# Batch 0 wholly by halves, one piece of zeros less, whole late stores, and a planner that may wait: a two-layer kernel on one core

## The chip, the cores and the metric

One Trainium2 chip; the program runs on one core of it. The time is device microseconds (us) of an execution; of several runs the median is given. The engines are called PE (TensorE, matrix products; PEld is its weight load), DVE (VectorE), ACT (ScalarE), POOL (GpSimd) and SP (SyncE, which here only starts transfers).

## What is computed

Eight batches of 256 tokens by 1024 features, all fp32. The first layer's weight matrix differs from batch to batch: a shared matrix plus a sign matrix, made of an integer mask, times the batch's coefficient. The second layer has one matrix for all batches and adds for each batch a low-rank adapter, chosen by the batch's number. Both layers have a bias and a residual.

```python
def _L0_cond_ref(hidden_states, W, b, coeff, mask):
    output = jnp.einsum('bsi,oi->bso', hidden_states, W) + b
    sign = (2 * mask - 1).astype(hidden_states.dtype)
    diff = jnp.einsum('bsi,bio->bso', hidden_states, sign)
    return output + diff * coeff[:, None, None]
...
def _L1_cond_ref(x, adapter_mapping, W, b, lora_As, lora_Bs):
    base_out = jnp.einsum('bti,oi->bto', x, W) + b
    A = lora_As[adapter_mapping]
    Bm = lora_Bs[adapter_mapping]
    lora_h = jnp.einsum('bti,bir->btr', x, A)
    lora_out = jnp.einsum('btr,bro->bto', lora_h, Bm)
    return base_out + lora_out * SCALING
x = x + _L0_cond_ref(x, L0_cond_W, L0_cond_b, condB_coeff, mask_Bx4096x4096_ik1)
x = x + _L1_cond_ref(x, itok_B_0_23, L1_cond_W, L1_cond_b, L1_cond_lora_As, L1_cond_lora_Bs)
```

Here x is 8 x 256 x 1024, the masks are 8 x 1024 x 1024 int32, and the adapters have rank 16.

## The kernel before, in words

Features lie on the 128 partitions, tokens in the free dimension. A weight matrix of 1024 x 1024 is cut into eight chunks of 128 input features (NC = 8) and two halves of 512 outputs (OH = 512).

**Batch 0** goes straight through, chunk by chunk. For each chunk SP loads the mask and the shared weights (lines 438 to 446) and parts of x (447 to 450); ACT makes the scaled signs of the mask (`convert`, line 403), DVE adds the identity for the residual into one 128 x 128 block and then the shared weights (`add`, line 314), and PE multiplies (line 494): 8 products of 256 columns per chunk. An fp32 product is two passes of PE, each with its weight load, so a chunk is 16 passes and the stage 128. Chunks 0 to 4 (`BY_HALF = 5`) are loaded, converted and added in halves of 512 outputs; for chunk 0 the first half is converted and added in quarters. Chunks 5 to 7 are taken whole: 512 KB per transfer, 1024 columns per conversion and per sum. The host lays the arrays of the chunks that go by halves so that each half is one contiguous piece.

**Batches 1 to 7** use Strassen's seven products with Winograd's sums (`seven`, products on line 680): weights in blocks (`block`, lines 403, 415 and 569), sums of blocks on DVE (line 314) and of tokens (line 665), the bias with the read of the accumulator on ACT (line 591). For batch 1 ACT first shifts the shared weights (line 415), and DVE multiplies the mask in (line 569).

**The second layer** runs for batches 0 to 3 after batch 3 and for batches 4 to 7 after batch 7 (`second_layer`), with seven outer times seven inner products (line 891) and the adapter's down and up products (lines 935 and 966). The first group keeps sums of weights in DRAM, and the second loads them again. Outputs are stored by POOL in the first group and by SP in the second. In the last group (`tail`) `store_halves` cuts a 256 KB store in two: for the four tiles of `c22`, and for the first tile of the last outer product (`done`). The last product of all is cut into three pieces (line 1062), each summed and stored at once.

**Before the first product** PE multiplies zeros (`idle`, lines 346 to 353): 256 and 128 columns, then a product of one row that spreads the coefficients over the partitions (line 362), then 256, 256 and 128 columns (line 368).

**The order of work** on the engines comes from a planner (class `Plan`). Each task has an engine, a guessed duration and perhaps a due time; PE's tasks keep the order in which they are written, and their nominal times add up in `plan.pe`. From these each task gets a latest start `ls`. `order` then simulates the engines: for every engine but PE it takes, of the tasks that can start now, the one with the smallest `ls`. For DVE and ACT (`idle` is true for these two alone) it also looks at tasks that become able while this one would run: if one of them is more urgent and this one is not due for over 3 us (`FAR`), it takes a shorter task that fits in front or waits:

```python
soon = [
    (u, v)
    for u, v in able
    if s < u < s + k.busy + self.MARGIN
    and v.ls < k.ls
    and v.ls < u + self.TIGHT
]
if soon and idle[e] and k.ls > s + self.FAR:
```

The transfers of the start have a fixed rank and so go out in the order in which they are written. The batch numbers (`itok`, 32 bytes) are loaded by SP; POOL reads them when it loads the adapters (line 847).

Of the kernel before, what the change touches and what calls it, by code (L numbers as in the profile page):

```python
# [9 lines left out]
I32 = mybir.dt.int32  # L10
# [3 lines left out]
P = 128  # L14
OH = 512
CG = 2
OQ = 256
BY_HALF = 5
DENSE = (0,)
EARLY = (1,)  # L20
SCALING = 2.0
# [32 lines left out]
class Plan:  # L54
# [60 lines left out]
    def order(self, slots, idle):  # L115
# [41 lines left out]
        while len(out) < len(self.tasks):  # L157
            best = None
            for e in free:
                if e == "PE":  # L160
                    if pe_at == len(pe) or pe[pe_at].open:
                        continue
                    k = pe[pe_at]
                    s = start(k)
                    if s is None:
                        continue
                    c = (s, k.ls, k)
                else:
                    able = [(s, k) for k in ready[e] if (s := start(k)) is not None]
                    if not able:  # L170
                        continue
                    t0 = min(s for s, _ in able)
                    s, k = min(((s, k) for s, k in able if s <= t0 + 0.02), key=lambda c: (c[1].ls, c[1].n))
# [4 lines that stand above are left out]
                        and v.ls < k.ls  # L178
                        and v.ls < u + self.TIGHT
                    ]  # L180
                    if soon and idle[e] and k.ls > s + self.FAR:
                        u = min(soon, key=lambda c: c[0])[0]
                        short = [
                            (a, v) for a, v in able if a <= t0 + 0.02 and a + v.busy <= u - self.MARGIN
                        ]
                        if short:
                            s, k = min(short, key=lambda c: (c[1].ls, c[1].n))
                        else:
                            s, k = min(soon, key=lambda c: (c[1].ls, c[1].n))
                    c = (s, k.ls, k)  # L190
                if best is None or c[:2] < best[:2]:
                    best = c
            if best is None:
                raise RuntimeError(
                    f"no place: {[(e, [k.n for k in v][:9]) for e, v in ready.items()]} at {free}, PE {pe_at}"
                )
            s, _, k = best
            e = k.engine
            for b in k.bufs:
                if b.kind and b.slot is None:  # L200
                    p = pick(b)
                    places[b.kind].remove(p)
                    b.slot = p[1]
            free[e] = s + k.busy
            end = s + k.busy + k.tail
            if k.bytes:
                lane = lanes["SW" if e == "POOL" else "HW"]
                at = max(s + k.busy + 0.5 * self.LATENCY[e], pipe)
                pipe = at + k.bytes / self.RATE
                end = pipe + 0.5 * self.LATENCY[e]  # L210
                lane.pop(0)
                lane.append(end)
            k.end = end
            for b in k.bufs:
                b.left -= 1
                b.end = max(b.end, end)
                if not b.left and b.kind:
                    places[b.kind].append([b.end + self.WAKE, b.slot, not b.partial])
            if e == "PE":
                pe_at += 1  # L220
            else:
                ready[e].remove(k)
            for a in k.after:
                a.open -= 1
                wake = 0.0 if a.engine == e and not k.bytes else self.WAKE
                a.ready = max(a.ready, (s + k.busy if a.engine == e and not k.bytes else end) + wake)
                if not a.open and a.engine != "PE":
                    ready[a.engine].append(a)
            out.append(k)
            k.done = True  # L230
            k.due = s
# [4 lines left out]
def kernel(  # L236
# [109 lines left out]
    def idle(*columns):  # L346
        def emit():
            for n in columns:
                nc.tensor.matmul(
                    idle_ps.t[:, 0, :n], lhsT=zeros[:, :P], rhs=zeros[:, :n], start=True, stop=True  # L350
                )

        pe(1, sum(columns) / 290, emit, (), (idle_ps((0,)),))
# [11 lines left out]
        (h_sb(h_rows), lb_pad((0, 1))),  # L365
        (c_ps((0,)),),
    )
    idle(T, T, T // 2)
    plan.pe = 5.2
    for o, f in ((two_c, 2.0), (neg_c, -1.0)):  # L370
        dve(
# [17 lines left out]
    def parts(c):  # L389
        every = slice(0, OH)  # L390
        if c == 0:
            return [(0, slice(0, OQ)), (0, slice(OQ, OH)), (1, every)]
        return [(0, every), (1, every)] if c < BY_HALF else [(None, every)]

    def halves(o):
        return tuple(q for q in range(2) if o.start < (q + 1) * OQ and o.stop > q * OQ)
# [21 lines left out]
        )  # L418

    w_b0 = [big(f"w_0_{c}", 2, OH) for c in range(NC)]  # L420
    w0_keys = lambda c, h: ((c, h),)

    def w_part(c, i, o):
        keys = tuple((i2, q) for i2 in (ALL if i is None else (i,)) for q in halves(o))
        sel = slice(0, 2) if i is None else slice(i, i + 1)
        return w_b0[c](keys, lambda t: t[:, sel, o])

    def w0_part(c, i, o):
        keys = tuple((c, i2, q) for i2 in (ALL if i is None else (i,)) for q in halves(o))
        sel = slice(0, 2) if i is None else slice(i, i + 1)  # L430
        return w0_sb(keys, lambda t: t[:, c, :].rearrange("p (h o) -> p h o", h=2)[:, sel, o])

    def first_loads(*load):
        k = dma(*load)
# [1 line left out]

    every = slice(0, OH)
    for c in range(NC):
        for i, o in [(0, every), (1, every)] if c < BY_HALF else [(None, every)]:
            n = P * (o.stop - o.start) * 4 * (1 if i is not None else 2)  # L440
            w = w_part(c, i, o)
            as_int = w.buf(w.keys, lambda t, f=w.index: f(t).bitcast(I32))
            src = lambda a: part(a, i)[:, o] if i is not None else a
            sel = lambda r: r if i is None else r.buf(r.keys, lambda t, f=r.index: f(t)[:, 0])
            for r, a in ((sel(as_int), mask[0, c]), (sel(w0_part(c, i, o)), w0T[c])):
                first_loads("SP", r, src(a), n)
            if c < 2 and i == 0:
                first_loads(("ACT", "SP")[c], x0_ref(0, c), part(x0T[0], c), P * T * 4)
            elif c and c % CG == 0 and i in (0, None):
                first_loads("SP", x0_ref(c // CG), x0T[c // CG], P * CG * T * 4)  # L450

    plan.task(
# [6 lines left out]
        due=4.2,  # L459
    )  # L460

    ident_keys = ((0,),)
    plan.task("POOL", 1.2, 0.1, lambda: make_identity(nc, ident.t), (), (ident((0,)),), due=6.0)

    def identity(c):
# [5 lines left out]
    for c in range(NC):  # L471
        h, q = divmod(c * P, OH)
        for i, o in parts(c):
            w = w_part(c, i, o)
            m = w.buf(w.keys, lambda t, f=w.index: f(t).bitcast(I32))
            n = (2 if i is None else 1) * (o.stop - o.start)
            convert(w, m, 0, n)
            if c >= 1 and i in (h, None) and o.start <= q < o.stop:
                d = w_b0[c](((h, q // OQ),), lambda t, h=h, q=q: t[:, h, q : q + P])
                add(d, d, ident((0,)), P)  # L480
            add(w, w, w0_part(c, i, o), n)
    for c in range(NC):
        for i, o in parts(c):
            ots = [
                h * TPH + j
                for h in (ALL if i is None else (i,))
                for j in range(o.start // P, o.stop // P)
            ]
            w = w_part(c, i, o)

            def emit(c=c, ots=ots):
# [49 lines left out]

    for ot in range(1, NC):
        read_dense(ot)
    dma("SP", itok_sb((0,)), itok, 32, due=50.0, ahead=20.0)

# [313 lines left out]
    def second_layer(group):  # L861
# [60 lines left out]
                due=plan.pe + due,  # L922
            )

        def store_halves(o, *where):
            for half in [slice(c, c + 1) for c in range(CG)] if tail else [slice(0, CG)]:
                store(o.buf(o.keys, lambda t, f=o.index, h=half: f(t)[:, h]), *where, c=half)

        def down():
            ph = bank(f"psh_{group}", 2, T, partial=True)  # L930

# [62 lines left out]
        class Run:  # L994
# [10 lines left out]

            def done(self, *uv):
                if self.dest:
                    whole = self.n + 1 < len(OUTER) or uv != (0, 0)
                    (store if whole else store_halves)(self.out[uv], *self.dest, *uv)
                if self.then:  # L1010
                    self.then(uv)

# [161 lines left out]
        for u in range(2):  # L1174
            o2, x2 = (q[u, 0].buf(ALL) for q in (c22, e1))
            add(o2, o2, x2, 1024, due=plan.pe + 5.0)
            for v in range(2):
                store_halves(c22[u, v], 1, 1, u, v)
        k.x2()
        k.y()  # L1180
        k.x3()
# [99 lines left out]
```

## Time and profile before

| what | value |
|---|---|
| three runs | 399.1, 399.93, 399.79 us; median 399.79 |
| the profiled execution | 399.8 us, span 398.1 |
| PE busy | 394.1 us (99%), 2752 passes |
| DVE, ACT, POOL busy | 327.7 (82%), 142.6 (36%), 44.5 us (11%) |
| batch 0's products (line 494) on the chain | 28.93 us, from 5.90 |
| batches 1 to 3 and 4 to 7 (line 680) on the chain | 75.04 us from 34.84, 100.05 us from 202.53 |
| transfers | 84.64 MB, mean 213 GB/s |

The page of the profile tells of one execution. Its chain of waits follows the work that ended last backwards: each step names an engine and a line of the kernel, or a transfer. The timeline lists instructions in order of time, like ones merged; a bracket holds the idle time of the engine ahead of an instruction and what ended it. A row of the windows view gives a stretch, its length, then busy us and instruction count of PE, PEld, DVE, ACT and POOL, PE's granted clock (1.00 is full), the share of time in which the transfer engines were busy, and GB/s. Matmuls overlap and their ends are modelled, so PE's pace is read from the starts.

### The profile page before, as it was taken

Reading aid. Unit: us, or ns where it says so; the run is one execution under the profiler, and the core shown is the slowest. Engines: PE = TensorE matmul, PEld = TensorE weight load, DVE = VectorE, ACT = ScalarE, POOL = GpSimd, SP = SyncE. Lnnn points to the kernel's source line nnn. Section 1 sums busy time; section 2 is a strip of 40 time slices with the busy share of each in tenths; the row PEclk is TensorE's granted clock in tenths of the full one; section 3 lists DMA queues with packets and bytes.
Section 4 is the critical chain, followed back from the end, with each engine's and each line's share of the span. In section 5 each row is a group of like instructions: output and inputs, shape, how many; then the busy total and the mean of one; then the engine's idle time right before and its main releaser. Section 6 shows DMA issues by size and latency. Waiting matters only on the chain.

```text
span 398.1 us, 6970 instructions
## 1 busy us (share of the span) xinstructions
PE 394.1 (99%) x2752; PEld 362.4 (91%) x2752; DVE 327.7 (82%) x417; ACT 142.6 (36%) x253; POOL 44.5 (11%) x87
## 2 busy tenths in 40 slices
PE   8999999999999999999999999999999999999997
PEld 7889999999978888888899999999998888888886
DVE  3559999999999999898999999999737366476475
ACT  5676675612043021017417366472212231110200
POOL 0000000132335331230233000000000000000000
DMA  7999998551558389679589665120001358555844
GB/s 278 395 403 410 406 408 341 179 193 53 194 197 283 150 281 344 209 246 323 174 303 335 198 227 192 53 54 28 0 28 54 115 151 243 173 143 182 272 125 160
DMA packets 31685, 84.64 MB, mean 213 GB/s; under 512 B 4388, under 2 KB 6308, under 8 KB 31652
## 3 DMA queue, kind: packets, MB, share of 16 engines
q1 hardware_dynamic: 25922, 67.19, 49.3%
q0 software_dynamic: 5440, 16.80, 11.3%
q8 instruction: 22, 0.36, 0.4%
q10 hardware_dynamic: 290, 0.20, 0.2%
q14 instruction: 11, 0.09, 0.1%
HBM read 64.25 MB, written 19.92 MB: 211 GB/s over the span
## 4 chain that ended last, share of the span: by engine, by line
PE 98%; DMA 1%; DVE 0%; SPq 0%; issue 0%; DVEq 0%
PE bank L680 44%; PE bank L891 42%; PE bank L494 7%; PE bank L966 2%; PE bank L935 2%; DMA w<-w0T 1%; PE bank L1062 0%; DVE big L314 0%; SPq L327 0%; DVEq L314 0%
## 5 line engine op out<-in xcount | busy, mean ns | idle before, releaser
L314 DVE TENSOR_TENSOR big<-big,big 128x1024 f32<-128x1024 f32 (+1 forms) x104 | 116.7, 1139 | 6.9 <-PE bank L680 4.4
L680 PE MATMUL bank<-small,big 128*128 128x128 f32 x896 | 103.3, 275 | 0.0
L680 PEld LDWEIGHTS bank<-small,big 128*128 128x128 f32 x896 | 101.7, 192 | 0.0
L314 DVE TENSOR_TENSOR big<-bank,big 128x512 f32<-128x512 f32 (+2 forms) x103 | 68.5, 677 | 37.3 <-PE bank L891 30.7
L891 PE MATMUL bank<-small,small 128*128 128x256 f32 x384 | 89.0, 380 | 0.0
L891 PEld LDWEIGHTS bank<-small,small 128*128 128x128 f32 x384 | 72.9, 190 | 10.6 <-issue 0.8
L680 PE MATMUL bank<-big,big 128*128 128x128 f32 x672 | 78.3, 275 | 0.0
L680 PEld LDWEIGHTS bank<-big,big 128*128 128x128 f32 x672 | 76.8, 192 | 0.1
L403 ACT ACTIVATE big<-big,neg_c,two_c 128x1024 f32<-128x1024 int32 (+2 forms) x62 | 69.5, 1162 | 12.3 <-DMA big<-mask 12.0
L314 DVE TENSOR_TENSOR big<-big,w 128x1024 f32<-128x1024 f32 (+2 forms) x62 | 67.4, 1117 | 5.8 <-ACT big L403 3.1
L591 ACT ACTIVATE big<-bank,b 128x128 f32<-128x128 f32 x112 | 32.0, 369 | 75.7 <-PE bank L680 66.2
L891 PE MATMUL bank<-big,small 128*128 128x256 f32 x224 | 52.5, 380 | 0.0
L891 PEld LDWEIGHTS bank<-big,small 128*128 128x128 f32 x224 | 42.4, 190 | 6.2 <-ACT big L318 0.7
L318 ACT COPY bank<-bank 128x512 f32<-128x512 f32 x20 | 11.4, 570 | 87.2 <-PE bank L891 61.8
L318 ACT COPY big<-bank 128x512 f32<-128x512 f32 x32 | 17.6, 593 | 56.7 <-PE bank L891 30.6
L494 PE MATMUL bank<-small,big 128*128 128x256 f32 x128 | 28.9, 390 | 0.2 <-DVE big L314 0.2
L494 PEld LDWEIGHTS bank<-small,big 128*128 128x128 f32 x128 | 25.1, 197 | 4.0 <-DVE big L314 0.5
L314 DVE TENSOR_TENSOR small<-big,small 128x512 f32<-128x512 f32 x35 | 23.8, 686 | 5.7 <-PE bank L891 5.6
L891 PE MATMUL bank<-big,big 128*128 128x256 f32 x112 | 26.7, 381 | 0.0
L891 PEld LDWEIGHTS bank<-big,big 128*128 128x128 f32 x112 | 21.1, 190 | 3.4 <-ACT big L318 0.7
L314 DVE TENSOR_TENSOR small<-big 128x512 f32<-128x512 f32 x21 | 14.4, 686 | 1.5 <-PE bank L891 1.5
L314 DVE TENSOR_TENSOR small<-big,big 128x512 f32<-128x512 f32 x21 | 14.4, 686 | 1.1 <-PE bank L891 1.1
(46 smaller groups left out, 163.9 us busy)
## 6 DMA issues: line engine op xcount, KB each, us to landing
big<-mask SPq DMA_DIRECT2D x59, 512.0 KB, 7.8
big<-xT SPq DMA_DIRECT2D x14, 512.0 KB, 5.8
big<-w1T SPq DMA_DIRECT2D x8, 512.0 KB, 5.5
leaf_S_s<-small POOLq DMA_DIRECT2D x16, 256.0 KB, 3.5
outT<-big POOLq DMA_DIRECT2D x16, 256.0 KB, 3.9
small<-leaf_S_s SPq DMA_DIRECT2D x16, 256.0 KB, 2.7
leaf_A_s<-small POOLq DMA_DIRECT2D x12, 256.0 KB, 2.7
leaf_S_a<-big POOLq DMA_DIRECT2D x12, 256.0 KB, 2.7
```

Of the source, the lines that this page charges most:

```text
L314: return dve(lambda: f(o.ap(), x.ap(), y.ap()), n, (x, y), (o,), due)
L318: "ACT", n / 1200 + 0.06, 0.11, lambda: nc.scalar.copy(o.ap(), x.ap()), (x,), (o,), due
L403: lambda: nc.scalar.activation(o.ap(), x.ap(), AF.Identity, bias=neg_c.t[:, b : b + 1], scale=two_c.t[:, b : b + 1]),
L494: nc.tensor.matmul(dense[ot // 2].t[:, ot % 2, :], lhsT=w_b0[c].t[:, h, j * P : (j + 1) * P], rhs=x0[c // CG].t[:, c % CG, :], start=c == ...
L591: lambda o=o, p=p, bias=bias: nc.scalar.activation(o.ap(), p.ap(), AF.Identity, bias=bias.ap()),
L680: nc.tensor.matmul(ps[:, j, :], lhsT=l[:, c, j * P : (j + 1) * P], rhs=m[:, 2 * a + c, :], start=first and a == 0 and c == 0 and j == 0, s ...
L891: nc.tensor.matmul(ps.t[:, j, :], lhsT=lt[:, c, j * P : (j + 1) * P], rhs=rt[:, c, :], start=start and c == 0 and j == 0, stop=False, skip ...
L935: nc.tensor.matmul(ph.t[i * S : i * S + R, 0, :], lhsT=la.t[:, i, c, :], rhs=y[GB * group + i, c // TPH].t[:, c % TPH, :], start=c == 0, s ...
L966: nc.tensor.matmul(ps[b].t[:, j, :], lhsT=lb_pad.t[rows, o : o + P], rhs=h_sb.t[rows, :], start=j == 0, stop=j == 1, skip_group_check=True,)
```

## The change

Five edits. Chunks 5 to 7 of batch 0 are taken by halves like the others, in the loads, the conversions, the sums and the layout that the host makes. The second series of zeros ends 128 columns earlier. The load of the batch numbers is issued by POOL. The stores that were cut in two go out whole. And the planner gets one more case: when the most urgent task k that could start now is due within 3 us, but a more urgent one becomes able while k would run, would be late behind k, and can itself be done before k is due, then the engine (DVE or ACT) waits for it.

```diff
-BY_HALF = 5
...
+                    late = [(u, v) for u, v in soon if v.ls < s + k.busy and u + v.busy <= k.ls]
+                    if late and idle[e] and k.ls <= s + self.FAR:
+                        s, k = min(late, key=lambda c: (c[1].ls, c[1].n))
-                    if soon and idle[e] and k.ls > s + self.FAR:
+                    elif soon and idle[e] and k.ls > s + self.FAR:
...
-    idle(T, T, T // 2)
+    idle(T, T)
...
-        return [(0, every), (1, every)] if c < BY_HALF else [(None, every)]
+        return [(0, every), (1, every)]
...
     for c in range(NC):
-        for i, o in [(0, every), (1, every)] if c < BY_HALF else [(None, every)]:
...
+        for i in range(2):
+            w = w_part(c, i, every)
+            m = w.buf(w.keys, lambda t, f=w.index: f(t).bitcast(I32))
+            first_loads("SP", m, part(mask[0, c], i), P * OH * 4)
+            first_loads("SP", w0_part(c, i, every), part(w0T[c], i), P * OH * 4)
...
-    dma("SP", itok_sb((0,)), itok, 32, due=50.0, ahead=20.0)
+    dma("POOL", itok_sb((0,)), itok, 32, due=50.0, ahead=20.0)
...
-        def store_halves(o, *where):
-            for half in [slice(c, c + 1) for c in range(CG)] if tail else [slice(0, CG)]:
-                store(o.buf(o.keys, lambda t, f=o.index, h=half: f(t)[:, h]), *where, c=half)
-
...
-                    whole = self.n + 1 < len(OUTER) or uv != (0, 0)
-                    (store if whole else store_halves)(self.out[uv], *self.dest, *uv)
+                    store(self.out[uv], *self.dest, *uv)
...
-                store_halves(c22[u, v], 1, 1, u, v)
+                store(c22[u, v], 1, 1, u, v)
...
-    for k in range(BY_HALF):
+    for k in range(D // P):
         by_part(arrays["mask"][0, k])
         by_part(arrays["w0T"][k])
```

More of the change, by code (lines that the diff above doesn't have):

```diff
@@ L420 @@
     w_b0 = [big(f"w_0_{c}", 2, OH) for c in range(NC)]
-    w0_keys = lambda c, h: ((c, h),)
     def w_part(c, i, o):
-        keys = tuple((i2, q) for i2 in (ALL if i is None else (i,)) for q in halves(o))
-        sel = slice(0, 2) if i is None else slice(i, i + 1)
-        return w_b0[c](keys, lambda t: t[:, sel, o])
+        return w_b0[c](tuple((i, q) for q in halves(o)), lambda t: t[:, i, o])
     def w0_part(c, i, o):
-        keys = tuple((c, i2, q) for i2 in (ALL if i is None else (i,)) for q in halves(o))
-        sel = slice(0, 2) if i is None else slice(i, i + 1)
-        return w0_sb(keys, lambda t: t[:, c, :].rearrange("p (h o) -> p h o", h=2)[:, sel, o])
+        return w0_sb(
+            tuple((c, i, q) for q in halves(o)),
+            lambda t: t[:, c, :].rearrange("p (h o) -> p h o", h=2)[:, i, o],
+        )
     def first_loads(*load):
@@ L438 @@
     for c in range(NC):
-        for i, o in [(0, every), (1, every)] if c < BY_HALF else [(None, every)]:
[L440 to L447, printed above, removed]
+        for i in range(2):
[3 more added lines that the diff above has]
+            first_loads("SP", w0_part(c, i, every), part(w0T[c], i), P * OH * 4)
+            if c < CG and i == 0:
                 first_loads(("ACT", "SP")[c], x0_ref(0, c), part(x0T[0], c), P * T * 4)
-            elif c and c % CG == 0 and i in (0, None):
+            elif c % CG == 0 and i == 0:
                 first_loads("SP", x0_ref(c // CG), x0T[c // CG], P * CG * T * 4)
@@ L460 @@
     )
-    ident_keys = ((0,),)
     plan.task("POOL", 1.2, 0.1, lambda: make_identity(nc, ident.t), (), (ident((0,)),), due=6.0)
@@ L475 @@
             m = w.buf(w.keys, lambda t, f=w.index: f(t).bitcast(I32))
-            n = (2 if i is None else 1) * (o.stop - o.start)
+            n = o.stop - o.start
             convert(w, m, 0, n)
-            if c >= 1 and i in (h, None) and o.start <= q < o.stop:
+            if c >= 1 and i == h and o.start <= q < o.stop:
                 d = w_b0[c](((h, q // OQ),), lambda t, h=h, q=q: t[:, h, q : q + P])
@@ L483 @@
         for i, o in parts(c):
[L484 to L488, printed above, removed]
+            ots = [i * TPH + j for j in range(o.start // P, o.stop // P)]
             w = w_part(c, i, o)
```

## The prediction

> **What bounds the kernel.** I read the chain of waits first, since it says which engine sets the end. Its columns are start, duration (both us) and what.
>
> ```profile
> 0.86 0.38 SPq L327
> 1.30 4.00 DMA w<-w0T
> 5.42 0.43 DVE big L314
> 5.90 28.93 PE bank L494 x128
> 34.84 75.04 PE bank L680 x672
> ...
> 393.51 1.77 PE bank L1062 x12
> 395.28 0.02 issue
> 395.30 0.29 DVE big L314
> ```
>
> From 5.90 to 395.28 the chain never leaves TensorE (PE). Ahead of it stand one transfer of weights that lands at 5.30 and one VectorE (DVE) sum; behind it one sum of 0.29, a store issued at 395.62 that lands at 397.19, and the closing steps up to 398.13. An edit therefore gains only if it makes PE start earlier, stop less, run faster, or shortens those last 2.8 us. The view of PE's waits names 0.2 us on data in the whole run. Weight loads wait 1.3 us in all, in four places, for ScalarE (ACT) copies; there successive matmuls start 0.30 apart instead of 0.216, so all four cost 4 x 0.09 = 0.4 us.
>
> So is anything left in PE's own time? The windows view counts matmul passes per stretch (a pass that crosses a border counts in both); a product has two passes.
>
> ```profile
> 6.90:7.90 1.00, 1.00 (x4) 0.80 (x3) 0.62 (x1) 0.58 (x1) 0.00 (x0) 1.00 1.08 389
> 8.90:9.90 1.00, 1.00 (x7) 0.87 (x6) 0.58 (x2) 0.74 (x1) 0.00 (x0) 1.00 1.04 377
> ```
>
> In narrow timeline windows, passes of 256 columns start at 4.61 and 5.04 (zeros), then 5.90, 6.49, 6.92, 7.34, 7.77 (batch 0), 0.43 apart, and from 8.12 on 0.216 apart. PE runs at half speed until about 8.05, while the column of granted clock says 1.00 throughout. The five passes from 5.90 to 8.12 take 2.22 us instead of 5 x 0.216 = 1.08, which loses **1.1 us**, the one sizeable loss in PE's 389 us. At the end of this stage PE lags behind its data, as these rows show for the last three chunks:
>
> ```profile
> 20.58 1.24 ACT L403 ACTIVATE big<-big,neg_c,two_c 128x1024 f32<-128x1024 int32 x1 [1.13 <-DMA big<-mask]
> 22.18 1.23 DVE L314 TENSOR_TENSOR big<-big,w 128x1024 f32<-128x1024 f32 x1
> 25.38 1.23 DVE L314 TENSOR_TENSOR big<-big,w 128x1024 f32<-128x1024 f32 x1 [0.66 <-DMA w<-w0T]
> 28.87 1.23 DVE L314 TENSOR_TENSOR big<-big,w 128x1024 f32<-128x1024 f32 x1
> ```
>
> Chunks 5, 6 and 7 are ready at 23.41, 26.61 and 30.10. PE takes 16 x 0.216 = 3.46 us per chunk and ends the stage at 34.84, so it begins them at 24.5, 27.9 and 31.4: each lies ready 1.1 to 1.3 us before its turn.
>
> **The parts.** The sum is made on the profiled execution, 399.8 us, of which 398.1 are span and 1.7 lie around it; the median of the three runs shown is 399.79 (399.1 to 399.93).
>
> *Chunks 5 to 7 by halves.* Loads: six transfers of 512 KB become twelve of 256 KB. SP issues six more, 0.33 us each, 2.0 us in all; but its 256 KB issues already stand 0.67 apart (13.21, 13.89, 14.58), waiting for earlier transfers, so issuing stays hidden. The windows view shows 395 GB/s in 14.9 to 20.0 (256 KB pieces) and 405 in 20 to 25 (512 KB). Moving 3.15 MB at the one rate instead of the other takes 7.97 against 7.78, so what is queued behind comes 0.2 us later. That is batch 1's masks and x. ACT: two conversions of 0.81 for one of 1.24, three times, +1.14 us. DVE: two sums of 0.69 for one of 1.23, three times, +0.45 us. Behind these in the queues are ACT's four 1.13 us weight shifts from 28.42 and DVE's mask products (1.28 each, from 30.02). The second of them ends at 33.76 and PE wants it at 36.46, so 2.7 us of cover stand against 0.2 + 0.45 + 1.14 = 1.8. Cost zero. The gain is zero too: a half chunk comes about 0.6 us earlier to an engine already 1.1 us behind. Without that cover the three costs would be paid in part, 0.45 (DVE alone) to 1.8.
>
> *One piece of zeros less.* It removes the passes started at 5.04 and 5.25. The weights land at 5.30 and their sum ends at 5.85, so these passes were not in the way of the product at 5.90: no direct gain. But PE then idles from 5.04 instead of 5.47 until 5.90: a gap of 0.86 instead of 0.43, just before the speed doubles. No row shows what gap the speed-up bears. In the trace, zeros restart at 3.17 after a broken stretch and full speed comes at 8.05, 4.9 us on. The upper bound is that the count starts anew at 5.90: full speed at 10.8, and the 2.75 us between at half speed, **+1.4 us**. The lower bound is zero: less activity gives no reason for an earlier speed-up. I take zero, since the nearest row, the break at 5.47 to 5.90, did not keep full speed from coming at 8.05; I keep both ends.
>
> [...]
>
> *The wait in the planner.* It holds DVE or ACT idle for a more urgent task instead of running one that is due within 3 us. What is held back is that task and everything behind it on the engine. DVE has no idle time to give between 34.8 and 127, as the windows show (DVE is the fourth number):
>
> ```profile
> 34.80:70.00 35.20, 35.20 (x318) 35.20 (x317) 34.83 (x35) 21.93 (x39) 0.00 (x0) 1.00 0.97 385
> 70.00:110.00 40.00, 40.00 (x360) 39.97 (x359) 39.90 (x52) 12.08 (x32) 12.51 (x23) 1.00 0.46 159
> ```
>
> The cover is DVE's lead. I matched the semaphore counts that products wait for with the times they were reached: between 35 and 110 most operands are ready 2 to 5 us before PE's turn; the closest are 0.9 (at 81.1), 1.1 (at 106.1) and 1.9 (at 47.2). One wait is at most the postponed task plus 0.3: 1.23 + 0.3 = 1.5 us of idle time. From below: PE has no waits to be cured but the 0.4 us named above. I take zero, because one short wait of 0.3 to 0.7 fits into the leads.
>
> *Late outputs whole.* Five pairs of 128 KB stores of the last group become five stores of 256 KB: five SP issues of 0.33 fewer, between 383 and 393. SP's last issues (393.14, 394.27, 394.86, 395.62) each come 0.02 after their own sum, so SP's time there is free. A 256 KB store lands 2.1 to 2.9 us after issue; issued at 390.8 it is done by 393.8, before the last store goes out at 395.62. Zero; without that cover a few tenths.
>
> *Batch numbers on GpSimd.* SP loses one issue of 0.30 at 32.47, GpSimd gains one (nearest row: a 4 KB load, 0.49, landing after 3.1). GpSimd waits 76.0 us until 77.4 and reads the numbers first then. Even issued behind the memset there, at 78.4, they would land at 81.5; the adapters' first product is at 113.3. Zero either way.
>
> Sum: 0 + 0 + 0 + 0 + 0, so **399.8**.
>
> **Rivals.** *A: no change that counts.* Chance 0.50. Small signs either way (0.2 on loads, 0.4 on copies) leave 399.1 to 400.5.
>
> *B: slower through the gap in the zeros*, ending on the other side. Place: PE, 5.04 to 5.90. It decides if the speed-up does not tolerate 0.86 us of idle time where it tolerated 0.43. Price 1.4: 401.2, by the bounds 400.6 to 401.6. For it: the break at 2.3 to 3.2 (between the first zeros and the restart at 3.17) is as long, and no full speed came within 4 us of the first zeros at 0.90. Against it: products at 5.90 follow at once and are activity themselves. Chance 0.28.
>
> *C: slower through DVE's order*: halves and new waits use up the closest lead, 0.9. Price: 0.45 + 0.2 + 1.5 - 0.9 = 1.25, or 401.0; more waits, up to 402. Chance 0.11.
>
> *D: faster.* If full speed comes earlier in the run, PE would reach chunk 5 about 1.1 us earlier, the moment it is ready; whole chunks would then hold PE back and halves would not. With the zeros out of the way of an early landing too, 1.1 is gained: 398.7, 398.3 to 399.0. For it: the runs shown spread by 0.8 us, and little but the start can vary. Against it: nothing in the diff hastens the start of this trace. Chance 0.11.
>
> *That the change does not do what it says*: the new condition may hold nowhere, and then the order of DVE and ACT stays. That is inside A.
>
> **How the numbers follow.** About 0.2% (0.8 us) is what a measurement of this kernel can tell from no change. Faster is D, 0.11; same is A, 0.50; slower is B and C, 0.39. The forecast is A's 399.8, whose own range is 399.1 to 400.5. The range of 8 in 10 takes in A and B and most of D: 398.7 to 401.6, leaving out C's far end and D's.
>
> **What would show it.** A: PE's chain again runs from about 5.9 to 395.3 with the batch 0 stage at 28.9 us. B: matmul passes still 0.43 apart after 8.5, and a batch 0 stage of 30 us or more. C: PE waits on DVE between 35 and 127, with idle time of DVE under the same lines. D: passes 0.216 apart before 7 us. The tail is right if the last store again goes out 0.02 after the last sum. What would make me wrong most cheaply is a first transfer that lands at another time than 5.30: it moves the end one for one.

## The result and the profile after

| | before | after |
|---|---|---|
| median of 22 executions each | 399.60 us | 400.27 us |
| lowest and highest | 399.02, 400.06 | 399.40, 401.74 |
| ratio, 95% interval | | 1.0019 (1.0012 to 1.0027) |
| profiled execution, span | 399.8, 398.1 us | 399.95, 398.0 us |

The changed kernel is slower by 0.7 us at the median, yet the profiled execution shows a span 0.1 us shorter. So the profile alone, read as before, explains nothing, and I begin with what it does show. The chain of waits of the changed kernel (start, duration, what; the kernel's lines have moved, and batch 0's products are now line 486, the sums line 316):

```profile
3.24 2.00 PE bank L351 x4
5.24 29.09 PE bank L486 x128
34.34 75.04 PE bank L672 x672
...
116.41 7.10 PE bank L883 x32
123.51 0.04 issue
123.55 1.99 PE bank L883 x8
...
395.09 0.02 issue
395.11 0.29 DVE big L316
```

PE still sets the end. In this execution the first weights landed 0.8 us earlier (at 4.52) than in the execution I had read before, so the first product starts at 5.12; that is luck. The stage of batch 0 takes 29.09 us on the chain, before 28.93. At 123.55 something new stands: PE's products start 0.42 us apart instead of 0.216, so 0.2 us is lost, and its weight load waits for a DVE sum. The first line is the kernel before, whose chain has no break there, the second the changed kernel's timeline:

```profile
116.91 8.83 PE bank L891 x40
```

```profile
123.55 1.59 PEld L883 LDWEIGHTS bank<-small,big 128*128 128x128 f32 x8 [0.44 <-DVE big L316]
```

Two windows of the changed kernel (columns as before):

```profile
8.90:9.90 1.00, 1.00 (x6) 0.87 (x5) 0.60 (x3) 0.81 (x1) 0.00 (x0) 1.00 1.03 393
34.80:70.00 35.20, 35.20 (x317) 35.20 (x317) 34.83 (x34) 22.83 (x39) 0.00 (x0) 1.00 0.98 389
```

DVE is as full as before, ACT works 0.9 us more in the second, and passes run at full speed in the first (0.216 us apart). The halves do what the edit says, two conversions and two sums per chunk (chunk 7's sums):

```profile
27.87 0.69 DVE L316 TENSOR_TENSOR big<-big,w 128x512 f32<-128x512 f32 x1 [1.12 <-ACT big L405]
...
29.94 0.69 DVE L316 TENSOR_TENSOR big<-big,w 128x512 f32<-128x512 f32 x1
```

**Where the time went** is seen when each execution's time is split into its span and what lies around it. I pool the executions of the changed kernel (the 22 above and the 11 of the first rerun below), and 99 of the kernel before, measured beside the experiments. Means: before 399.63 = 397.97 + 1.66, after 400.36 = 398.26 + 2.09 (rounded). Of the 0.73 us, **0.43 lie around the span and 0.29 in it**. Around the span, the kernel before has 1.61 to 1.71 in every execution; the changed one has over 1.85 in 18 of 33, up to 3.24. The prediction took the 1.7 us as a constant.

### The profile page after: what moved, and what is told of

It reads as the page before. It is cut to its first block, busy times and chain, and to the rows that moved or that the text cites. A ratio compares the mean times of both kernels' runs of the same rounds, so it can differ in the third digit from the quotient of the medians.

```text
span 398.0 us, 6960 instructions
## 1 busy us (share of the span) xinstructions
PE 394.1 (99%) x2750; PEld 361.5 (91%) x2750; DVE 328.0 (82%) x420; ACT 144.0 (36%) x256; POOL 45.1 (11%) x88
## 4 chain that ended last, share of the span: by engine, by line
PE 99%; DVE 0%; issue 0%
PE bank L672 44%; PE bank L883 42%; PE bank L486 7%; PE bank L954 2%; PE bank L923 2%; PE bank L351 1%; PE bank L1049 0%; PE bank L364 0%; DVE big L316 0%
## 5 line engine op out<-in xcount | busy, mean ns | idle before, releaser
L405 ACT ACTIVATE big<-big,neg_c,two_c 128x1024 f32<-128x1024 int32 (+2 forms) x65 | 71.1, 1123 | 10.7 <-DMA big<-mask 10.6
```

Source lines behind the costliest of these rows:

```text
L405: lambda: nc.scalar.activation(o.ap(), x.ap(), AF.Identity, bias=neg_c.t[:, b : b + 1], scale=two_c.t[:, b : b + 1]),
```

## The experiments

Each ran in 7 to 12 executions beside 29 to 35 of the kernel before. "Around" is the time less the span.

### One edit alone, on the kernel before

**Zeros.** `idle(T, T, T // 2)` becomes `idle(T, T)`.

> The kernel before with one edit alone: the second series of zeros ends 128 columns earlier. Theory T (the longer gap ahead of the first product makes PE's full speed come later in a part of the executions): ratio 1.001 to 1.003, with some executions 1 to 1.5 us above the rest and batch 0's products taking 30 us or more in those. Rival R1 (the added time comes from GpSimd's early transfer) and rival R2 (it comes from the planner's new order on DVE): ratio 1.000, within 0.0007.

Ratio 1.0010 (1.0001 to 1.0019); mean span 398.39, around 1.73 (at most 1.81). T's size fits, but its sign is absent: no group of executions stands 1 us above the rest (399.48 to 400.72 without a break). In the profile batch 0's products took 29.9 us, but began 0.7 us earlier than in the profile before. And 0.24 us were lost at 197.7, where PE waits for a DVE sum that the planner had put elsewhere: changing the guessed length of the zeros moved DVE's order too. The same order, with the same 0.24 us, stands in the profile of the kernel with the zeros in fewer products below.

**Batch numbers.** `dma("SP", itok_sb...` becomes `dma("POOL", itok_sb...`.

> The kernel before with one edit alone: GpSimd issues the load of the batch numbers. T and R2: ratio 1.000, within 0.0007. R1: 1.001 to 1.002, of which the larger part lies around the span, since the changed kernel's runs show up to 3.2 us around the span where the profiled ones show 1.7.

Ratio 1.0006 (0.9998 to 1.0015), around 1.61 to 1.71: R1's sign is absent. GpSimd issues the load at 1.6 us, since nothing stands ahead of it, and it delays nothing visible. The execution profiled here shows another thing: full speed came at 7.0 us instead of 8.05, and then PE was held back by whole chunks.

```profile
23.95 3.32 PEld L494 LDWEIGHTS bank<-small,big 128*128 128x128 f32 x16 [0.42 <-DVE big L314]
...
28.21 6.77 PEld L494 LDWEIGHTS bank<-small,big 128*128 128x128 f32 x32 [0.94 <-DVE big L314]
```

The brackets are the weight loads' idle time at chunks 5 and 6; between matmul starts 0.2 and 0.7 us were lost. That is the mechanism of rival D: full speed came early and whole chunks held PE back.

**Planner.**

```diff
+                    late = [(u, v) for u, v in soon if v.ls < s + k.busy and u + v.busy <= k.ls]
+                    if late and idle[e] and k.ls <= s + self.FAR:
+                        s, k = min(late, key=lambda c: (c[1].ls, c[1].n))
-                    if soon and idle[e] and k.ls > s + self.FAR:
+                    elif soon and idle[e] and k.ls > s + self.FAR:
```

> The kernel before with one edit alone: the planner's new case. T and R1: ratio 1.000, within 0.0007. R2: 1.0005 or more; the trace shows a matmul start 0.4 instead of 0.216 after the one before it, waiting for DVE between 35 and 130 us, as at 123.55 in the changed kernel, where it costs 0.2 us. If the order holds the same waits as before, 1.000 for R2 too.

Ratio 0.9998 (0.9989 to 1.0007), after 10 us no stall of PE that the kernel before does not have. Alone it costs nothing.

**Halves.** `BY_HALF = 5` becomes `BY_HALF = 8`.

> The kernel before with one edit alone: chunks 5 to 7 of batch 0 by halves too. All three theories: ratio 1.000, within 0.0007; the operands of batch 1's products are ready up to 1 us later than before against their turn, and PE still does not wait. If whole chunks held PE back in executions in which its full speed comes early, 0.999.

Ratio 1.0007 (0.9998 to 1.0015), span 398.27, within what was expected and not told apart from nothing. PE waited 0.08 us at 81.1 and 0.07 at 124.0.

**Whole stores.** `if tail else [slice(0, CG)]` becomes `if False else [slice(0, CG)]`.

> The kernel before with one edit alone: the five halved stores of the last group go out whole. All theories: ratio 1.000 within 0.0007, the last store again issued 0.02 us after the last sum. If whole stores delay the last small ones on the transfer engines, 1.0005 or more, with the last store landing later than 1.6 us after its issue.

Ratio 1.0016 (1.0008 to 1.0025), mean span 398.52: a clear miss, by an edit that I had costed at nothing. What the expectation's last sentence allowed for came true. From the last sum's end to the end of the span it takes 2.96 us, before 2.54. At the end SP waits for the stores to land. This is its view of waits from 394 us on, first of the kernel before, then of this one (waits in total, their number, the longest):

```profile
SPq L327 <- DVE big L314: 1.6, 3, 0.7
SPq L1276 <- DMA outT<-big: 0.7, 3, 0.3
```

```profile
SPq L327 <- DVE big L314: 1.6, 3, 0.7
SPq L1276 <- DMA outT<-big: 1.1, 3, 0.6
```

Two things make it longer. The last 64 KB store lands 1.69 us after its issue instead of 1.57 (1.65 to 1.66 in the changed kernel). And SP tests the eight semaphores of its transfers one after another, 0.06 us each, always in the same order; every transfer takes the next of the eight in turn. Before, the last store happened to hold the eighth, and all others had been tested when it landed. With five transfers fewer it holds the third, and five tests follow: 5 x 0.06 = 0.3. All 14 profiles fit this within 0.03 us:

| version | transfers of SP, against before | last store's place | last sum to end of span |
|---|---|---|---|
| halved stores: before, zeros, planner, two more below | 0 | 8th | 2.53 to 2.54 us |
| batch numbers | -1 | 7th | 2.59 |
| halves | +6 | 6th | 2.66 |
| whole stores | -5 | 3rd | 2.96 |
| changed kernel (+6 - 1 - 5), and its versions | 0 | 8th | 2.62 to 2.63 |
| changed kernel, batch numbers by SP | +1 | 1st | 3.02 |

So the step costs 0.06 for each place short of the eighth, and whole stores cost 0.09 to 0.12 besides. In the changed kernel the places cancel by chance and only the 0.09 is left.

### The changed kernel again, and without one edit

> The changed kernel itself, once more, to be measured beside three versions that each lack one edit. Theory S (the edits cost a little each, mostly by the start: zeros 0.001, halves and batch numbers 0.0007 and 0.0006, planner nothing): ratio 1.0015 to 1.0025, with the time around the span near 1.7 us as in the single edits. Rival R (the edits together lengthen what lies around the span): 2 us or more around it in half of the executions, and the span itself only 0.2 us longer.

Ratio 1.0015 (1.0005 to 1.0024). Around: 1.67 to 1.70 in five executions, 2.09 to 2.77 in six. That is R's sign.

**Zeros put back**, `idle(T, T, T // 2)`:

> The changed kernel with the 128 columns of zeros put back. S: 0.0005 to 0.0015 less than the changed kernel in the same runs, full speed of PE by 8.8 us at the latest in the profile. R: the same as the changed kernel.

Ratio 1.0006 (0.9997 to 1.0015), around 1.63 to 1.80. The lengthening is gone. (Full speed came at 8.95, 0.15 later than S allowed.)

**Batch numbers by SP again:**

> The changed kernel with the batch numbers loaded by SP again. S: 0.0003 to 0.0008 less than the changed kernel. R, if GpSimd's early transfer is what lengthens the time around the span: that time is back at 1.65 to 1.7 us, and the ratio 0.001 less than the changed kernel's.

Ratio 1.0025 (1.0015 to 1.0036): slower, not faster. Both theories miss. Around is still up to 2.80, so GpSimd's transfer is not its cause; the span grew by 0.5, of which 0.40 is the last store in the first place of the eight. In this profile full speed came at 7.5, and PE gave 0.6 us back at 123.85, waiting for DVE.

**The old planner:**

> The changed kernel with the old planner. S: the same as the changed kernel within 0.0007; the matmul start that comes 0.42 after the one before it at 123.55 is gone (0.2 us), which is less than this measurement tells. R: the same. If the planner's new case with the other edits costs more than the trace shows, 0.001 less.

Ratio 1.0037 (1.0025 to 1.0049) with 7 executions, span 398.86. Also a miss: with the other edits the new case helps. One stall can be shown. DVE's timeline without the new case, and then with it, around the read of an accumulator that PE needs:

```profile
194.81 0.69 DVE L313 TENSOR_TENSOR big<-bank,big 128x512 f32<-128x512 f32 x1
195.53 1.23 DVE L313 TENSOR_TENSOR big<-big,big 128x1024 f32<-128x1024 f32 x1
196.68 0.68 DVE L313 TENSOR_TENSOR big<-bank,big 128x512 f32<-128x512 f32 x1
```

```profile
194.64 0.69 DVE L316 TENSOR_TENSOR big<-bank,big 128x512 f32<-128x512 f32 x1
195.54 0.69 DVE L316 TENSOR_TENSOR big<-bank,big 128x512 f32<-128x512 f32 x1 [0.22 <-PE bank L883]
196.15 1.82 DVE L316 TENSOR_TENSOR big<-big,big 128x1024 f32<-128x1024 f32 x2
```

With the old planner DVE starts a 1.23 us sum, the read comes at 196.68, and PE's next product starts 0.24 us late, at 197.41. With the new one DVE idles 0.22 us, reads at 195.54, and PE's operand is ready 0.75 us before its turn. This is the edit as it was meant; it explains 0.24 of the 0.6 us between the two mean spans (with 0.10 more at the next product, 0.34), and the rest stays open. This is the stall of the zeros alone (197.7) once more. It stands in all three profiles that have the shorter zeros and the old planner, and in none of the other eleven: one edit brings it, another removes it.

### What lies around the span

All versions with the long time around share one thing. PE's program has 5575 instructions in the changed kernel and in its versions with the old planner and with the batch numbers by SP, but 5579 or more in all others (the traces record two fewer of each), and the profile's instruction queue 8 shows one transfer less for it. The changed kernel's rerun, then the kernel before:

```profile
q8 instruction: 21, 0.34, 0.4%
```

```profile
q8 instruction: 22, 0.36, 0.4%
```

22 transfers of 16 KB over PE's 5583 recorded instructions are 65 bytes each, so this queue seems to bring PE's code. The page counts within the span. In the kernel before the 22nd block is fetched at 390.7 us. In the rerun the trace holds it at 400.3, 1.8 us after the end of the span, taking 1.24 us, and this execution has 2.65 around its span. (The trace of the changed kernel's first profile, with 1.93 around, holds no 22nd block at all.) Four traces hold the late block, the fourth that of the kernel with zeros in fewer products below (us):

| version | block's end, after the span's end | around the span | difference |
|---|---|---|---|
| changed kernel, rerun | 3.02 | 2.65 | 0.37 |
| batch numbers by SP | 3.15 | 2.78 | 0.37 |
| zeros in fewer products | 2.95 | 2.58 | 0.37 |
| old planner | 1.89 | 1.66 | 0.24 |

Where an execution's time begins and ends in the trace is not known, so the 0.37 itself says nothing. That it is the same three times does: the time ends at a fixed distance from the block's end, as it should if the end waits for the block. In the fourth the block came early enough: 1.89 less 0.37 is under the usual 1.66, and nothing is added. Two kernels test whether the length of the program alone does it.

**One product more.** The change in the first series of zeros, ahead of the coefficients:

```diff
-    def idle(*columns):
+    def idle(*columns, extra=()):
         def emit():
-            for n in columns:
+            for n in columns + extra:
...
-    idle(T, T // 2)
+    idle(T, T // 2, extra=(1,))
```

> The changed kernel with one product of zeros more, one column wide, in the first series ahead of the coefficients: PE's program grows by 4 instructions, from 5575 to 5579, and DVE's, ACT's, GpSimd's and SP's stay the same; the 128 columns ahead of the first real product stay away. Theory F (PE's program has become so short that its last 16 KB of code are fetched after the last product instead of before it, and the end waits for that): the last transfer of the instruction queue is back at about 391 us, the time around the span at 1.6 to 1.8 us in all executions, the ratio to the kernel before 1.0003 to 1.001. Rival G (the wider gap in the zeros itself lengthens what lies around the span): the time around the span is over 2 us in about half of the executions, as in the changed kernel, and the ratio 1.0015 to 1.0025.

Ratio 1.0007 (0.9998 to 1.0016), around 1.62 to 1.78 in all 11, the last code transfer at 391.7. F holds, G falls.

**The same zeros in fewer products**, on the kernel before with the shorter zeros:

```diff
-    zeros = nc.const_aps.tensor(0.0, [P, T], F32)
+    zeros = nc.const_aps.tensor(0.0, [P, 2 * T], F32)
...
-    idle(T, T // 2)
+    idle(T + T // 2)
...
-    idle(T, T)
+    idle(2 * T)
```

> The kernel before with the second series of zeros 128 columns shorter, as measured already, and the same zeros in two products instead of four (384 and 512 columns): PE's program shrinks from 5581 to 5573 instructions, the other engines' stay the same. F: the time around the span is over 2 us in about half of the executions, where it was 1.63 to 1.81 with 5581 instructions, the last code transfer comes at about 400 us, and the ratio rises from 1.001 to 1.0015 to 1.0025. G: the time around the span stays at 1.6 to 1.8 us, ratio 1.001.

Around rose from at most 1.81 to as much as 2.61, over 1.85 in 5 of 12, and the last code transfer came at 400.1, as F said. But only 2 of 12 are over 2 us, where F said about half, and the ratio, 1.0013 (1.0005 to 1.0022), lies under F's 1.0015 and is not told apart from the 1.0010 of the kernel with 5581 instructions. The split into span and around is what decides: in none of the versions with 5579 instructions or more is an execution over 1.81.

**More work for DVE**, to test rival C: for batch 2 the sum of tokens `t1` is made three times.

```diff
+        def again(n, x, z):
...
         token_sum("t1", tokens(0, 1), tokens(0, 0))
+        if b == 2:
+            again("t1", tokens(0, 1), tokens(0, 0))
+            again("t1", tokens(0, 1), tokens(0, 0))
```

> The kernel before with three sums of tokens (128x512, 0.69 us each) on DVE where there was one, for batch 2: 1.37 us of DVE work more near 65 us, nothing more for PE. Theory C (DVE is so full from 35 to 127 us that work added there soon holds PE back, as the stalls at 123.5 to 123.9 in the versions by halves suggest): PE stalls by 0.4 to 0.8 us between 80 and 128 us, ratio 1.001 to 1.0018. Rival (PE's lag behind DVE absorbs it): no such stall, ratio 1.000 within 0.0007.

Ratio 1.0001 (0.9992 to 1.0010), no stall: C falls for added work of this size. DVE had no room between 35 and 127 us and yet did it: the stage from 127 to 178 shows where the less urgent sums went, before and with the added work.

```profile
127.00:178.00 51.00, 51.00 (x272) 44.37 (x264) 48.13 (x71) 7.25 (x14) 16.05 (x30) 1.00 0.72 250
```

```profile
127.00:178.00 51.00, 51.00 (x272) 44.34 (x264) 49.22 (x72) 7.26 (x14) 16.17 (x30) 1.00 0.71 250
```

1.09 of the 1.37 us came there, where DVE has room. So what makes PE wait at 123.5 to 123.9 is probably not DVE's sum of work but its order; the order was not changed by itself. It shows where PE is early: waits there stand in the four profiles in which batch 1's products begin earliest, at 34.07 to 34.47 us (changed kernel 0.2 us, batch numbers by SP 0.6, halves and whole stores 0.07), and in none of the ten in which they begin at 34.53 or later. The profile with the added work is one of those ten (34.73), so by itself it does not test an early PE.

## Why the prediction was right or wrong

**The forecast.** No change that counts, 399.8, held: 400.27 is in its own range and the ratio 1.0019 within the 0.2%, though the interval reaches over it. But it held because the costs are small, not because its sum of zeros was right: that left out two real costs.

- **The 1.7 us around the span**, carried over as a constant, was the step that failed. It is 0.43 us larger on average, 0.6 of the whole, by a mechanism that none of the rivals had. Removing the zeros took 4 instructions from PE, the other edits six waits (both counted in the traces), which left 5575, and the last block of code was then fetched after the work. Shown by taking it away and by making it.
- **Whole stores at zero** was wrong. I asked only whether the last store would be issued on time. It was, but it lands 0.09 to 0.12 later, and what comes after the landing depends on the number of transfers. 0.09 remains in the changed kernel, 0.4 when the edit is alone.
- **Zeros: "not in the way"** was right for the one execution that I read and wrong in general. Its weights landed late; in all six other profiles with the longer zeros, PE starts the first product at 5.46, as the zeros end, though the sum is done by 5.2. Without them it starts at 5.1 to 5.3. This gain of 0.26, 5.46 less the mean of 5.20, I had put into rival D alone.
- **Rival B** cost nothing like its price, and its condition was never met. The gap of 0.86 us assumed the late weights; in all seven profiles with the shorter zeros the first product comes 0.02 to 0.24 us after the zeros' last pass has had its time, so a gap of 0.86 remains untested. Full speed came at 6.9 to 8.95 in the seven profiles with the longer zeros (mean 8.1) and at 7.45 to 9.65 in the seven with the shorter (mean 8.7). 0.6 us later at half loss is 0.3, not 1.4, and the earlier start gives 0.26 back. With such a spread even the 0.6 is not settled. All 14 profiles, with either length of zeros, lie between 6.87 and 9.65, and the two groups overlap, so the spread looks like chance; what sets it, no run shows. Nor does any run show the 1.8 us by which the far end of B's range, 401.6, lies above 399.8: the latest full speed, 9.65, is 1.6 us after the 8.05 of before, 0.8 us at half loss.
- **Halves at zero, and D.** D's mechanism is real: where full speed came early, whole chunks held PE back by 0.9 us (batch numbers) and 0.2 us (whole stores). The halves let PE through, and then DVE's order holds it at 123.5 to 123.9 (0.2 us in the changed kernel, 0.6 with SP's batch numbers). So the gain is given back 90 us later, and I had not looked what is late next.
- **Planner and batch numbers** cost nothing alone that can be told from zero (ratios 0.9998 and 1.0006), as said; that the planner's case would repair a stall that the shorter zeros bring was not foreseen.

Of the 0.29 us in the span, 0.09 is the tail. The other 0.2 lies between the start and DVE's order and cannot be split with one profile per version.

## What to carry to other kernels

When one engine is busy 99% of the span, look at the time outside the span and behind the last instruction as closely as at the work: the split of each execution into the two found here what no chain of waits shows. An edit that changes how many instructions or transfers a program has moved the end here by 0.06 to 0.5 us on average through the place of a code block or of the last semaphore. Such an edit should be tried again with a few instructions of padding before it is called better or worse. One profiled execution is a sample of the start: read several before saying what is in the way.

## What was not expected of the hardware

In these runs the end of an execution seems to wait for code: with 5573 or 5575 instructions on PE, the fetch of the 22nd block of 16 KB began 0.6 to 1.8 us after the end of the span in four profiles, and up to 1.5 us were added in about half of the executions; with 5579 or more it came at 390.6 to 391.8 us and at most 0.1 was added. In the one profile in which it began 0.6 us after the span (old planner), 1.66 lie around it: that fetch was early enough to cost nothing. What decides when it comes, and where between 5575 and 5579 the border lies, stays open. At the end SP tests its semaphores here in a fixed order, 0.06 us each, so that the place of the last store among eight decides up to 0.4 us.
